# A four-layer vision kernel: the stage between two selective scans, with its turned images in a pool of their own

## Chip, cores and metric

The kernel runs on 1 core of one Trainium2 chip. The metric is the device time of one execution in microseconds (us), the median of several runs; lower is better.

## What is computed

The input is `x`, 4 images of 64 x 64 pixels with 192 channels, in float32. Four layers are applied in turn, each as `x = x + layer(group_norm(x))`. Layers 0 and 3 are two-dimensional selective scans ("ss2d"); layer 1 is a Mamba block over rows and columns, layer 2 a Toeplitz mixer. The change lies in layers 0 and 3. Cut to what matters, layer 0 is (layer 3 is the same with 192 instead of 384 inner channels):

```python
xz = x @ in_proj_w.T
xp, z = xz[..., :DI], silu(xz[..., DI:])
xc = silu(depthwise_conv3x3(xp) + conv_b)         # the "u" of the scans
xs = [rows(xc), columns(xc), reversed rows, reversed columns]
delta = softplus(...);  Bs, Cs = ...               # small projections of xs
h = exp(delta * A) * h + (delta * u) * B           # along 4096 positions, 16 states
y = sum over states of h * C, + D * u
y = y of the four ways, each turned back, summed
y = layer_norm(y) * gamma + beta
out = (y * z) @ out_proj_w.T
```

## The kernel before

**Layout.** An image lies as 96 partitions x 2 x 4096 pixels (`x`), the inner channels as `P` partitions x `NT` tiles: 128 x 3 in layer 0, 96 x 2 in layer 3. A chunk is `T` = 512 pixels, 8 rows; an image has `NCH` = 8 chunks.

**Order of the work.** `build` computes `both_weights` (weights of layer 1 multiplied out: 24 products on TensorE, stored to DRAM), then layer 0, layer 1, layer 2, layer 3. In each of layers 0 and 3, `ss2d` runs five "between" stages and four scans in turn: `ss2d_between(b)` makes the input of image b beside the output of image b-1, then `ss2d_scan` scans image b. The first between stage has no output, the last no input.

**Who orders instructions.** The kernel is written with a tile framework: the program says which tile each instruction reads and writes, pools give tiles their places in on-chip memory, and a planner orders each engine's instructions beforehand and puts in the waits. Each engine then runs its list strictly in order; SyncE (SP) and ScalarE and GpSimd hold DMA queues that are lists of the same kind. Pools are stacked from the left end of memory, or from the right one with `side="right"`; a pool that is closed leaves its place to later ones, which have to wait until its tiles are done with.

**Input** (`ss2d_input`, L550-645). Pool "a" on the left holds `pad`, the image with a border. Pool "a_u" (on the left behind it) holds `by_col`, the turned image of one tile (one buffer, 16 KB per partition), `one` (4 buffers of 2 KB) and `o` (2 of 16 KB). Pool "a_x" on the right holds `x`. `x` is loaded (L570), normalised (L103) and projected on TensorE (`in_ps`, L593) into `pad` (L597). Then the convolution: the last tile by nine products per chunk on TensorE (`conv_ps`, L612), Silu (`one`, L614), turned on GpSimd (L615); the other tiles by nine passes on VectorE (`o`, L622 and L624), Silu (L627), turned as a whole on GpSimd (L632). Rows go to DRAM as `u_d[0]` (L616, L628), the turned image as `u_d[1]` from SP's queue (L635). The turned image of tile NT-2, the last one made, is stored by a function `late` that `ss2d_input` returns.

**Output** (`ss2d_output`, L736-820), eight chunks from the last to the first. Pool "o_in" on the right (2 buffers) holds `acc` (the row result of the scans), `u` and `xr`, the image; `cols` on the left holds all column results. Its own tiles lie in pools "o", "o_stats" and "o_turn" on the left, where "a" and "a_u" were. Per chunk:

- `xn` is `xr` normalised (L103), `z` its projection (`zp`, L760) through Silu (L764)
- `acc` gets D times `u` (L766) and the columns (L771)
- the mean over channels is a product (`mean`, L774); it is subtracted from `acc` in place (L775); Square into `sq` (L777, 2 buffers), `var` (L780), then Ln and Exp (L782, L783)
- `acc` is scaled, shifted and gated in place (L784, L786, L789)
- the output product (`op`, L794) reads `acc`, and `xo` (L797) adds `xr`
- `xo` is stored (L798); in layer 0 it is also turned on GpSimd (`turned`, L802) for layer 1
- the loads of the chunk two further on are issued (`fetch`, L61)

In layer 0, for images 0 and 1, the statistics of image b+2 are counted here too, in four loads of 1024 pixels (`peek`, L812, 2 buffers; `count`, L77).

**Scan** (`ss2d_scan`). For each of four ways and each chunk it loads `u` from `u_d[col]`, projects it (`xd_ps`, L226) and scans (VectorE, L428/L435; products with C on GpSimd, L439). The ways come in the order columns, rows, columns reversed, rows reversed; the reversed ways add what the forward ones stored (`earlier`).

Of the kernel before, what the change touches and what calls it, by code (L numbers as in the profile page):

```python
# [7 lines left out]
F32 = mybir.dt.float32  # L8
AF = mybir.ActivationFunctionType
# [5 lines left out]
C = 192  # L15
# [21 lines left out]
class Kernel:  # L37
# [436 lines left out]
    def ss2d(self, pre, x_in, x_out, P, NT, ways, bias_twice, counted, turn):  # L474
# [4 lines left out]
        with tc.tile_pool(name=f"{pre}lay", bufs=1) as lay:  # L479
            w = {"counted": counted, "turn": turn}  # L480
            for name in ("in_w", "conv_w", "conv_b"):
                w[name] = self.load(lay, name, ins[pre + name])
            taps = w["taps"] = lay.tile([P, 9, P], F32, name="taps")
            w["nm"] = lay.tile([PC, B, KC, 2], F32, name="nm")
            A = self.load(lay, "A", ins[f"{pre}A"])
            D = self.load(lay, "D", ins[f"{pre}D"])
            dtb = self.load(lay, "dtb", ins[f"{pre}dt_b"])
            for name in ("gamma", "beta", "out_w"):
                w[name] = self.load(lay, name, ins[pre + name])
            avg = w["avg"] = lay.tile([P, P], F32, name="avg")  # L490
# [12 lines left out]

            for b in range(B + 1):
                self.ss2d_between(b, x_in, x_out, u_d, y_d, P, NT, w, begin if b == 0 else None)
                if b < B:
                    self.ss2d_scan(pre, u_d[b], y_d[b], P, NT, ways, A, dtb)

    def ss2d_between(self, b, x_in, x_out, u_d, y_d, P, NT, w, begin):
# [3 lines left out]
        with ExitStack() as ctx:  # L513
# [25 lines left out]
            if b < B:  # L539
                late = self.ss2d_input(b, x_in, u_d[b], P, NT, w, begin, ahead)  # L540
            else:
                ahead()
                late = None
            if last is not None:
                self.ss2d_output(last, x_in, x_out[last], P, NT, w, cols, loads, late)
            elif late is not None:
                late()
            aside.close()

    def ss2d_input(self, b, x_in, u_d, P, NT, w, begin, ahead):  # L550
# [5 lines left out]
        with (  # L556
            tc.tile_pool(name="a", bufs=1) as pa,
            tc.tile_pool(name="a_u", bufs=2) as pu,
            tc.tile_pool(name="a_ps", bufs=4, space=PSUM) as psum,
# [6 lines left out]
            with tc.tile_pool(name="a_x", bufs=1, side="right") as px:  # L566
# [22 lines left out]
                for t in range(NT):  # L589
                    for c in range(NCH):  # L590
# [9 lines left out]
                        )  # L600
            ahead()
            for t in [NT - 1, *range(NT - 1)]:
                by_col = pu.tile([P, HW, HW], F32, name="by_col", bufs=1)
                turned = by_col.rearrange("p b a -> p a b")
                bias = cb[:, t : t + 1]
                if t == NT - 1:
                    for c in range(NCH):
                        rows = slice(c * ROWS, (c + 1) * ROWS)
                        ps = psum.tile([P, ROWS, HW], F32, name="conv_ps", tag="mm")
                        for j in range(9):  # L610
                            win = pad[:, t, c * ROWS + j // 3 : (c + 1) * ROWS + j // 3, j % 3 : j % 3 + HW]
                            nc.tensor.matmul(ps, taps[:, j, :], win, start=j == 0, stop=j == 8)  # L612
                        one = pu.tile([P, ROWS, HW], F32, name="one", bufs=4)
                        nc.scalar.activation(one, ps, AF.Silu, bias=bias)  # L614
                        nc.gpsimd.tensor_copy(turned[:, rows, :], one)  # L615
                        nc.sync.dma_start(u_d[0][:, t, c * T : (c + 1) * T], one.rearrange("p a b -> p (a b)"))  # L616
                else:
# [14 lines left out]
                    nc.gpsimd.tensor_copy(turned, o)  # L632

                def late(t=t, by_col=by_col):
                    nc.sync.dma_start(u_d[1][:, t, :], by_col.rearrange("p a b -> p (a b)"))  # L635

                if t != NT - 2:
                    late()
            if fresh:
# [4 lines left out]
                self.moments(nm[:, 1], self.mv[:, 1], pa, psum)  # L644
        return late

    def ss2d_scan(self, pre, u_d, y_d, P, NT, ways, A, dtb):
# [3 lines left out]
        with (  # L651
# [26 lines left out]

            for k, (col, rev) in sorted(enumerate(ways), key=lambda one: (one[1][1], not one[1][0])):
                w = {"dtb": dtb[:, k, :], "A": A[:, k]}  # L680
# [54 lines left out]

    def ss2d_output(self, b, x_in, x_out, P, NT, w, cols, loads, late):  # L736

# [4 lines left out]
        with (  # L742
# [8 lines left out]
            for at, c in enumerate(range(NCH - 1, -1, -1)):  # L751
# [21 lines left out]
                for t in range(NT):  # L773
                    nc.tensor.matmul(mean, avg, acc[:, t, :], start=t == 0, stop=t == NT - 1)  # L774
                nc.vector.tensor_sub(acc, acc, mean.unsqueeze(1).broadcast_to([P, NT, T]))  # L775
                sq = po.tile([P, NT, T], F32, name="sq")
                nc.scalar.activation(sq, acc, AF.Square)  # L777
                var = psum.tile([P, T], F32, name="var")
# [4 lines left out]
                nc.scalar.activation(rstd, rstd, AF.Exp, scale=-0.5)  # L783
                nc.vector.tensor_mul(acc, acc, rstd.unsqueeze(1).broadcast_to([P, NT, T]))  # L784
                for t in range(NT):
                    nc.scalar.activation(  # L786
                        acc[:, t, :], acc[:, t, :], AF.Identity, bias=be[:, t : t + 1], scale=g[:, t : t + 1]
                    )
                nc.vector.tensor_mul(acc, acc, z)  # L789
                xo = po.tile([PC, KC, T], F32, name="xo")  # L790
                for m in range(KC):
                    op = psum.tile([PC, T], F32, name="op", tag="op")
                    for t in range(NT):
                        nc.tensor.matmul(  # L794
                            op, ow[:, t, m * PC : (m + 1) * PC], acc[:, t, :], start=t == 0, stop=t == NT - 1
                        )
# [9 lines left out]
                if at + 2 < NCH:  # L806
                    loads["fetch"](c - 2)
                if at == 0 and late is not None:
                    late()
# [12 lines left out]
    def both_weights(self):  # L822

        nc, ins = self.nc, self.i
        P, NT = 128, 3
        both_w = [self.dram.tile([P, NT, C], F32, name=f"m_both_w{i}") for i in range(4)]
        with (
            self.tc.tile_pool(name="n", bufs=2) as pn,
            self.tc.tile_pool(name="n_ps", bufs=2, space=PSUM) as psum,
        ):  # L830
            fw = self.load(pn, "fw", ins["L1_fc_w"], bufs=1)
            for i, part in enumerate((4, 6, 0, 2)):
# [9 lines left out]
                nc.sync.dma_start(both_w[i], both)  # L842
        return both_w

# [368 lines left out]
def build(tc, ins, out):  # L1213
    with ExitStack() as ctx:
        k = Kernel(ctx, tc, ins, out)
        x0 = [ins["x"][b] for b in range(B)]
        x1, x3 = (k.image_tiles(n) for n in ("x1_", "x3_"))
        both_w = k.both_weights()
        turned = k.image_tiles("turned")
        k.ss2d("L0_", x0, x1, 128, 3, ROW_COL, False, False, turned)  # L1220
        k.toeplitz(x1, k.mamba(x1, turned, both_w), x3)
        k.ss2d("L3_", x3, [out[b] for b in range(B)], 96, 2, ROW_ROW, True, True, None)
# [122 lines left out]
```

## Time and profile before

| | |
|---|---|
| median of 3 runs | 30774.61 us (30773.04 to 30777.48) |
| the profiled execution | 30801.53 us, its span 30799.7 us |
| granted TensorE clock in it | 0.963 of full speed |
| scans of layer 0 (first to last scan on VectorE) | 214-2496, 2882-5165, 5548-7828, 8186-10469 us |
| scans of layer 3 | 24844-26077, 26359-27592, 27875-29108, 29390-30624 us |
| convolution on TensorE (L612), each | 62 us |
| first to last `xo` of an output stage | 164 to 180 us in layer 0, 116 to 118 us in layer 3 |

A row of a list of groups or a timeline reads: engine, line, operation, output<-inputs, shapes; times are in us, a mean in ns. A row of waits reads: who waited at which line, "<-" for what, then the total, the times and the longest. In rows of stretches, each engine has its busy time and number of instructions; PEclk is the granted TensorE clock. PE is TensorE, DVE VectorE, ACT ScalarE, POOL GpSimd, SP SyncE; a "q" behind a name is its queue, PEld the weight loads.

### The profile page before, as it was taken

Reading aid. Unit: us, or ns where it says so; the run is one execution under the profiler, and the core shown is the slowest. Engines: PE = TensorE matmul, PEld = TensorE weight load, DVE = VectorE, ACT = ScalarE, POOL = GpSimd, SP = SyncE. Lnnn points to the kernel's source line nnn. Section 1 sums busy time; section 2 is a strip of 40 time slices with the busy share of each in tenths; the row PEclk is TensorE's granted clock in tenths of the full one; section 3 lists DMA queues with packets and bytes.
Section 4 is the critical chain, followed back from the end, with each engine's and each line's share of the span. In section 5 each row is a group of like instructions: output and inputs, shape, how many; then the busy total and the mean of one; then the engine's idle time right before and its main releaser. Section 6 shows DMA issues by size and latency. Waiting matters only on the chain. (4 is left out here: it accounts for less than half of the span.)

```text
span 30799.7 us, 503679 instructions
## 1 busy us (share of the span) xinstructions
PE 26995.3 (88%) x189440; PEld 15772.5 (51%) x189440; DVE 22446.6 (73%) x16865; ACT 23230.3 (75%) x50324; POOL 22912.2 (74%) x9903
## 2 busy tenths in 40 slices
PE   8998998899899888888888888888588988888888
PEld 5664665566466444444444444444355445444444
DVE  7886888788788677777777777777433367676777
ACT  6885886788688688888888888888222278888888
POOL 6885886788588599989998999999100068787877
PEclk9999999999999999999999999999788999999999
DMA  3333333333333333333333333333533445454444
GB/s 108 97 105 112 96 103 112 101 98 104 112 96 102 106 97 97 98 99 101 101 103 98 97 97 98 101 101 101 132 83 72 110 116 135 123 135 124 131 126 126
DMA packets 1644091, 3276.35 MB, mean 106 GB/s; under 512 B 395797, under 2 KB 452566, under 8 KB 1627574
## 3 DMA queue, kind: packets, MB, share of 16 engines
q1 hardware_dynamic: 1533110, 3076.28, 36.7%
q10 hardware_dynamic: 108544, 167.85, 1.6%
q8 instruction: 1497, 24.53, 0.3%
q14 instruction: 940, 7.70, 0.1%
HBM read 2121.50 MB, written 618.33 MB: 89 GB/s over the span
## 5 line engine op out<-in xcount | busy, mean ns | idle before, releaser
L395 PE MATMUL b<-diag,dtuT 128*64 128x256 f32 x98304 | 12600.0, 386 | 1753.8 <-DVE h L428 928.1
L439 POOL TENSOR_TENSOR hc<-h,c 128x1024 f32<-128x1024 f32 x4608 | 10947.5, 2395 | 2001.2 <-DVE h L435 1401.3
L395 PEld LDWEIGHTS b<-diag,dtuT 128*64 128x64 f32 x98304 | 8177.8, 138 | 6281.2 <-DVE h L428 1920.3
L418 ACT ACTIVATE dA<-both,A 128x512 f32<-128x512 f32 (+1 forms) x12288 | 8304.6, 716 | 2111.5 <-DVE h L428 1462.7
L435 DVE TENSOR_TENSOR_SCAN h<-dA,carry,b 128x512 f32<-128x512 f32 x6720 | 8170.0, 1264 | 1355.5 <-PE b L395 827.8
L439 POOL TENSOR_TENSOR h<-h,c 128x1024 f32<-128x1024 f32 x3072 | 7221.2, 2373 | 1058.6 <-DVE h L428 884.4
L349 ACT ACTIVATE diag<-ident,bt 128x128 f32<-128x128 f32 x20480 | 6617.8, 396 | 91.9 <-issue 91.3
L464 PE MATMUL y<-hc,fold 128*64 128x512 f32 x18432 | 5771.0, 599 | 383.9 <-POOL hc L439 382.2
L428 DVE TENSOR_TENSOR_SCAN h<-dA,b 128x1024 f32<-128x1024 f32 x2304 | 5204.5, 2275 | 1147.2 <-ACT dA L418 801.2
L368 POOL TENSOR_TENSOR bs<-dtu,bc 128x1024 f32<-128x1024 f32 x1536 | 3640.1, 2370 | 46.2 <-DMA c<-bc_dram 33.2
L464 PE MATMUL y<-h,fold 128*64 128x512 f32 x12288 | 3256.3, 593 | 8.9 <-POOL h L439 8.9
L464 PEld LDWEIGHTS y<-hc,fold 128*64 128x64 f32 x18432 | 1897.3, 138 | 1576.9 <-POOL hc L439 812.2
L428 DVE TENSOR_TENSOR_SCAN h<-b,bs 128x1024 f32<-128x1024 f32 x768 | 1759.1, 2290 | 1028.2 <-ACT b L418 728.9
L418 ACT ACTIVATE b<-both,A 128x504 f32<-128x504 f32 (+1 forms) x3072 | 2087.6, 680 | 360.0 <-DVE h L435 322.1
L563 POOL MEMSET pad<- 128x396 f32 (+1 forms) x8 | 7.7, 967 | 3093.3 <-DMA in_w<-in_L_in_w 2997.8
L435 DVE TENSOR_TENSOR_SCAN h<-b,carry,bs 128x512 f32<-128x512 f32 x1344 | 1639.9, 1261 | 234.4 <-issue 131.0
L254 PEld LDWEIGHTS dtu_ps<-ident,dtu 128*64 128x64 f32 (+1 forms) x16384 | 1173.6, 141 | 491.4 <-issue 365.3
L464 PEld LDWEIGHTS y<-h,fold 128*64 128x64 f32 x12288 | 1007.2, 137 | 787.2 <-issue 444.6
L435 DVE TENSOR_TENSOR_SCAN h<-dA,b 128x512 f32<-128x512 f32 x960 | 1112.1, 1206 | 374.2 <-PE b L395 196.2
L418 ACT ACT_TABLE_LOAD x1019 | 1307.4, 1283 | 13.3 <-DMA c<-bc_dram 1.6
L254 PE MATMUL dtu_ps<-ident,dtu 128*64 128x128 f32 (+1 forms) x16384 | 1263.0, 272 | 45.5 <-DVE dtu L295 41.2
L937 DVE SCALAR_TENSOR_TENSOR u<-in_ps,conv_w,u 128x504 f32<-128x504 f32 (+2 forms) x1152 | 832.5, 723 | 405.9 <-ACT u L932 396.8
(165 smaller groups left out, 25106.1 us busy)
## 6 DMA issues: line engine op xcount, KB each, us to landing
c<-bc_dram SPq DMA_DIRECT2D x3072, 256.0 KB, 4.1
both<-delta SPq DMA_DIRECT2D x2048, 128.0 KB, 2.8
bc<-bc_dram SPq DMA_DIRECT2D x768, 256.0 KB, 4.1
both<-delta_dram SPq DMA_DIRECT2D x1536, 128.0 KB, 3.5
dtu<-dtu_dram SPq DMA_DIRECT2D x1536, 128.0 KB, 2.6
dtu<-dtu SPq DMA_DIRECT2D x1280, 128.0 KB, 2.5
L_y<-out ACTq DMA_DIRECT2D x512, 256.0 KB, 3.1
u<-L_u SPq DMA_DIRECT2D x160, 768.0 KB, 5.5
```

Source lines behind the costliest of these rows:

```text
L254: nc.tensor.matmul(to[half * 64 : (half + 1) * 64], of[:, half * 64 : (half + 1) * 64], self.ident[:p, :p], start=True, stop=True,)
L349: nc.scalar.activation(to, self.ident, AF.Copy, scale=of)
L368: self.nc.gpsimd.tensor_mul(by(b), dtu, by(job["bbc"][p]))
L395: nc.tensor.matmul(to, dtu, job["diag"][p][:, k, 2 * q : 2 * q + 2, :], start=True, stop=True,)
L418: nc.scalar.activation(to[n], of, AF.Exp, scale=w["A"][:, g, 2 * p + n : 2 * p + n + 1])
L428: nc.vector.tensor_tensor_scan(h[:, way], dA[:, way], b[:, way], 0.0, ALU.mult, ALU.add)
L435: nc.vector.tensor_tensor_scan(hn[:, n, way], dA[:, n, way], by_n[:, n, way], start, ALU.mult, ALU.add)
L439: nc.gpsimd.tensor_mul(hc, h, job["cbc"][p])
L464: nc.tensor.matmul(y[c * 64 : (c + 1) * 64, :], self.fold, of, start=first == 0 and n == 0, stop=last == LAST and n == 1)
L563: nc.gpsimd.memset(pad[:, :, 0 : S : S - 1, :], 0.0)
L937: nc.vector.scalar_tensor_tensor(u[:, :, to], ps[:, :, of], tap(3 - j), u[:, :, to], ALU.mult, ALU.add)
```

## The change

- `a_u` is opened on the right side, after `ahead()` has opened "o_in" there; `one` has 3 buffers instead of 4.
- The turned images are stored from GpSimd's queue, each as soon as it is made; `late` is gone.
- The centred sum is a tile `yc` of its own (2 buffers); `acc` is no more written after the mean. `sq` has one buffer.
- `peek` is one buffer of 512 pixels, loaded eight times, one or two chunks per output chunk.
- The ways are ordered rows, columns, columns reversed, rows reversed.
- `both_weights` runs after the first between stage of layer 0 instead of ahead of it, in a pool on the right.

```diff
             for b in range(B + 1):
                 self.ss2d_between(b, x_in, x_out, u_d, y_d, P, NT, w, begin if b == 0 else None)
+                if b == 0 and turn is not None:
+                    self.both_weights()
...
-            tc.tile_pool(name="a_u", bufs=2) as pu,
...
             ahead()
+            pu = right.enter_context(tc.tile_pool(name="a_u", bufs=2, side="right"))
...
-                        one = pu.tile([P, ROWS, HW], F32, name="one", bufs=4)
+                        one = pu.tile([P, ROWS, HW], F32, name="one", bufs=3)
...
-                def late(t=t, by_col=by_col):
-                    nc.sync.dma_start(u_d[1][:, t, :], by_col.rearrange("p a b -> p (a b)"))
-
-                if t != NT - 2:
-                    late()
+                nc.gpsimd.dma_start(u_d[1][:, t, :], by_col.rearrange("p a b -> p (a b)"))
...
-            for k, (col, rev) in sorted(enumerate(ways), key=lambda one: (one[1][1], not one[1][0])):
+            for k, (col, rev) in sorted(enumerate(ways), key=lambda one: (one[1][1], one[1][0] != one[1][1])):
...
-                nc.vector.tensor_sub(acc, acc, mean.unsqueeze(1).broadcast_to([P, NT, T]))
-                sq = po.tile([P, NT, T], F32, name="sq")
-                nc.scalar.activation(sq, acc, AF.Square)
+                yc = po.tile([P, NT, T], F32, name="yc")
+                nc.vector.tensor_sub(yc, acc, mean.unsqueeze(1).broadcast_to([P, NT, T]))
+                sq = po.tile([P, NT, T], F32, name="sq", bufs=1)
+                nc.scalar.activation(sq, yc, AF.Square)
...
-                nc.vector.tensor_mul(acc, acc, rstd.unsqueeze(1).broadcast_to([P, NT, T]))
+                nc.vector.tensor_mul(yc, yc, rstd.unsqueeze(1).broadcast_to([P, NT, T]))
...
-                nc.vector.tensor_mul(acc, acc, z)
+                nc.vector.tensor_mul(yc, yc, z)
...
-                if at == 0 and late is not None:
-                    late()
-                if peek is not None and at < NCH // 2:
-                    one = po.tile([PC, KC, 2 * T], F32, name="peek")
-                    nc.sync.dma_start(one, x_in[peek][:, :, 2 * at * T : 2 * (at + 1) * T])
-                    for i in range(2):
-                        self.count(ahead, one[:, :, i * T : (i + 1) * T], 2 * at + i)
-                elif peek is not None and at == NCH // 2 + 1:
+                for i in () if peek is None else (0, 1) if at == 0 else (at + 1,) if at < NCH - 1 else ():
+                    one = po.tile([PC, KC, T], F32, name="peek", bufs=1)
+                    nc.sync.dma_start(one, x_in[peek][:, :, i * T : (i + 1) * T])
+                    self.count(ahead, one, i)
+                if peek is not None and at == NCH - 2:
                     self.sum_up(self.mv[:, peek], ahead)
...
-            self.tc.tile_pool(name="n", bufs=2) as pn,
+            self.tc.tile_pool(name="n", bufs=2, side="right") as pn,
...
-        both_w = k.both_weights()
```

More of the change, by code (lines that the diff above doesn't have):

```diff
@@ L539, in ss2d_between @@
             if b < B:
-                late = self.ss2d_input(b, x_in, u_d[b], P, NT, w, begin, ahead)
+                self.ss2d_input(b, x_in, u_d[b], P, NT, w, begin, ahead)
             else:
                 ahead()
-                late = None
             if last is not None:
-                self.ss2d_output(last, x_in, x_out[last], P, NT, w, cols, loads, late)
-            elif late is not None:
-                late()
+                self.ss2d_output(last, x_in, x_out[last], P, NT, w, cols, loads)
             aside.close()
@@ L644, in ss2d_input @@
                 self.moments(nm[:, 1], self.mv[:, 1], pa, psum)
-        return late
     def ss2d_scan(self, pre, u_d, y_d, P, NT, ways, A, dtb):
@@ L734, in ss2d_scan, with ss2d_output @@
             self.run_jobs(jobs, pools)
-    def ss2d_output(self, b, x_in, x_out, P, NT, w, cols, loads, late):
+    def ss2d_output(self, b, x_in, x_out, P, NT, w, cols, loads):
         tc, nc = self.tc, self.nc
@@ L783, in ss2d_output @@
                 nc.scalar.activation(rstd, rstd, AF.Exp, scale=-0.5)
-                nc.vector.tensor_mul(acc, acc, rstd.unsqueeze(1).broadcast_to([P, NT, T]))
+                nc.vector.tensor_mul(yc, yc, rstd.unsqueeze(1).broadcast_to([P, NT, T]))
                 for t in range(NT):
                     nc.scalar.activation(
-                        acc[:, t, :], acc[:, t, :], AF.Identity, bias=be[:, t : t + 1], scale=g[:, t : t + 1]
+                        yc[:, t, :], yc[:, t, :], AF.Identity, bias=be[:, t : t + 1], scale=g[:, t : t + 1]
                     )
-                nc.vector.tensor_mul(acc, acc, z)
+                nc.vector.tensor_mul(yc, yc, z)
                 xo = po.tile([PC, KC, T], F32, name="xo")
@@ L794, in ss2d_output @@
                         nc.tensor.matmul(
-                            op, ow[:, t, m * PC : (m + 1) * PC], acc[:, t, :], start=t == 0, stop=t == NT - 1
+                            op, ow[:, t, m * PC : (m + 1) * PC], yc[:, t, :], start=t == 0, stop=t == NT - 1
                         )
@@ L807, in ss2d_output @@
                     loads["fetch"](c - 2)
-                if at == 0 and late is not None:
-                    late()
-                if peek is not None and at < NCH // 2:
-                    one = po.tile([PC, KC, 2 * T], F32, name="peek")
-                    nc.sync.dma_start(one, x_in[peek][:, :, 2 * at * T : 2 * (at + 1) * T])
-                    for i in range(2):
-                        self.count(ahead, one[:, :, i * T : (i + 1) * T], 2 * at + i)
-                elif peek is not None and at == NCH // 2 + 1:
+                for i in () if peek is None else (0, 1) if at == 0 else (at + 1,) if at < NCH - 1 else ():
[3 more added lines that the diff above has]
+                if peek is not None and at == NCH - 2:
                     self.sum_up(self.mv[:, peek], ahead)
@@ L825, in both_weights @@
         P, NT = 128, 3
-        both_w = [self.dram.tile([P, NT, C], F32, name=f"m_both_w{i}") for i in range(4)]
+        both_w = self.both_w = [self.dram.tile([P, NT, C], F32, name=f"m_both_w{i}") for i in range(4)]
         with (
-            self.tc.tile_pool(name="n", bufs=2) as pn,
+            self.tc.tile_pool(name="n", bufs=2, side="right") as pn,
             self.tc.tile_pool(name="n_ps", bufs=2, space=PSUM) as psum,
@@ L842, in both_weights @@
                 nc.sync.dma_start(both_w[i], both)
-        return both_w
     def mamba(self, x_in, by_col, both_w):
@@ L1217, in build @@
         x1, x3 = (k.image_tiles(n) for n in ("x1_", "x3_"))
-        both_w = k.both_weights()
         turned = k.image_tiles("turned")
         k.ss2d("L0_", x0, x1, 128, 3, ROW_COL, False, False, turned)
-        k.toeplitz(x1, k.mamba(x1, turned, both_w), x3)
+        k.toeplitz(x1, k.mamba(x1, turned, k.both_w), x3)
         k.ss2d("L3_", x3, [out[b] for b in range(B)], 96, 2, ROW_ROW, True, True, None)
```

## The prediction

> **What bounds the kernel now.** I read the page first, for where time is lost at all.
>
> ```profile
> PE 26995.3 (88%) x189440; PEld 15772.5 (51%) x189440; DVE 22446.6 (73%) x16865; ACT 23230.3 (75%) x50324; POOL 22912.2 (74%) x9903
> ```
>
> Every engine is busy most of the time because the scans fill 27 of 30.8 ms. The change leaves the scans' instructions alone; it touches the stages between them. So I split the span by the first and last scan of each image in the timeline: in layer 0 DVE scans nothing in 0-214, 2496-2882, 5165-5548, 7828-8186 and 10469-10775 us; in layer 3 in 26077-26359, 27592-27875, 29108-29390 and from 30624 to the end, 30800. These holes (and the start of layer 3, 24697-24844) are what the change can win or lose: some 2500 us.
>
> Next, one hole in stretches: layer 0, input of image 1 beside output of image 0.
>
> ```profile
> core 0: us, PE busy (x) PEld busy (x) DVE busy (x) ACT busy (x) POOL busy (x), PEclk, DMA share, GB/s
> 2546.00:2608.00 62.00, 62.00 (x145) 27.01 (x143) 61.97 (x20) 14.26 (x13) 19.05 (x7) 1.00 0.43 142
> 2608.00:2649.00 41.00, 5.48 (x13) 2.20 (x12) 4.38 (x3) 0.69 (x1) 15.24 (x3) 0.60 0.56 227
> 2693.00:2739.00 46.00, 37.92 (x74) 14.63 (x73) 26.64 (x25) 21.13 (x24) 3.66 (x4) 0.87 0.27 84
> 2739.00:2800.00 61.00, 43.65 (x78) 16.54 (x77) 29.84 (x28) 23.05 (x26) 7.77 (x4) 0.78 0.24 75
> ```
>
> The convolution (row 1) fills PE. Then 41 us in which PE works 5.5. Then the output's eight chunks, in pairs of 46 to 61 us, where no engine is full and PE is nearest. The waits of 2608-2650 name the owner of the dead stretch:
>
> ```profile
> ACT sq L777 <- DMA L_u<-by_col: 40.5, 1, 40.5
> DVE xn L103 <- DMA L_u<-by_col: 33.4, 1, 33.4
> POOL by_col L632 <- DMA L_u<-by_col: 18.7, 2, 12.3
> ```
>
> xn and sq do not read by_col; they wait because their pool "o" lies on the place of the closed pool "a_u". by_col has one buffer, so the end is a serial chain on POOL: store, copy 7.08 us, store, copy, store. Tiles at the bottom of "o" wait too, although only its top reaches a_u, so the wait is by pool. The check: in layer 0's third hole (no peek tile, "o" 16 KB smaller, ending inside the old pad) the first zp starts at 7943.7, right after the convolution's 7942.3. There is no stall there.
>
> The two starts, from the waits of 150-214 and 0-45 us:
>
> ```profile
> PE xd_ps L226 <- DMA u<-L_u: 40.4, 1, 40.4
> DVE stats L77 <- DMA m_both_w<-both_w: 27.5, 1, 27.5
> ```
>
> The first scan reads turned columns, stored last (u loaded at 186.65); and the first statistics wait until both_weights' pool is free. Last, a pair of layer 3's output, from the timeline:
>
> ```profile
> 27776.49 0.31 SPq L61 DMA_DIRECT2D acc<-L_y  x1
> 27780.05 0.75 DVE L766 SCALAR_TENSOR_TENSOR acc<-u,Dsum,acc 96x512 f32<-96x512 f32 x1 [0.29 <-DMA acc<-L_y]
> 27784.16 1.99 PE L774 MATMUL mean<-acc,avg 96*96 96x512 f32 x2 [3.40 <-issue]
> 27792.28 1.22 DVE L775 TENSOR_TENSOR acc<-acc,mean 96x1024 f32<-96x1024 f32 x1 [1.22 <-PE mean L774]
> 27807.10 6.85 PE L794 MATMUL op<-acc,out_w 96*96 96x512 f32 x8 [5.92 <-DVE acc L789]
> ```
>
> acc's slot is free only when op has read it, so the load of the chunk two on is issued at op's end, and load, sum, mean (15.8 us to the subtraction at 27792.28) stand in series with the rest of every pair.
>
> **The change, part by part.**
>
> *By_col on the right (own pool, GpSimd stores).* From the tile sizes in KB per partition, layer 0: base 16, cols 48, pad 52 end at 116. The new "o" (xn 8, z 12, yc 12, sq 6, rstd 4, xo 8, peek 4) runs from 64 to 118. From the top: o_in 32, a_u 54 (by_col 16, one 6, o 32). With about 208 KB usable (the Trainium skill, "SBUF — State Buffer", section "SBUF size: 192, 224, or 256?"; no row shows it) a_u is 122 to 176: clear of "o". Layer 3: "o" ends near 82, a_u starts near 130. So the wait goes; next late is the convolution itself. What it is worth: from the convolution's end to the first op, holes 1 and 2 of layer 0 take 67.0 us (2608.1 to 2675.1), hole 3 takes 28.6 (7942.3 to 7970.9): 38.4 each, 77. In layer 3 it is 42.0, 42.0 and 40.9; without the wait, the 18.6 from xn to op (26198.7 to 26217.3) plus 4.5 of mean and subtraction that now sit inside the stall, about 23.5: 18 each, 55.
> Turned (32 KB on top of "o") still meets a_u, so GpSimd's first L802 waits for the last store, about 2650; xo is first due near 2642 and its buffer again a pair (42 us) later, so nothing waits. Bounds for this part: 132 gained, or 100 if the first output pair is slowed by DVE's tail.
>
> *Stores on GpSimd's queue.* SP's issue of one costs 0.32 us and it lands 6.3 us later (2 MB); three stores (layer 3: two) leave SP in each hole, worth about 1 us. Behind GpSimd's store stand only the next by_col copy, which needs that store anyway, and turned. No row shows a GpSimd store. A rule speaks against it: the Trainium skill, "SBUF — State Buffer", section "SBUF: two separate sides", says that such a store's descriptors are written by GpSimd, which is locked out while DVE runs a two-port operation. The nearest row: GpSimd's by_col copy takes 1.04 us alone and up to 5.27 beside DVE's taps (one tap pass 4.47). In the holes the first such store comes after DVE's taps (2600.7 against 2610.0), so row and rule both give 0; only at layer 0's start could it wait, some 4.5 us a store, and there rows go first. I take 0; bounds -2 and +5 a hole.
>
> *Right-hand a_u over x.* At layer 0's start peek holds the top 32 KB, so a_u lies on x, and in layer 3 o_in is only 24 KB. By the pool-wide wait above, DVE's taps now start when in_ps ends: +26.7 us at layer 0's start (61.8 to 88.5), +13 in layer 3. In layer 3 the convolution covers it (taps would end at 26157, PE at 26175). At layer 0's start it is not covered.
>
> *both_weights moved, rows first.* Start of layer 0: without the 27.5 us wait, the statistics follow x (its last part took 17 us from issue in hole 1, behind some 4 us of weight loads), ending near 27 instead of 38.65: 12 earlier. in_ps ends 76.5, taps (78.7 us, 61.8 to 140.5) end 155, Silu of the first rows and their store make u loadable at about 160.5 instead of 186.65: 26 gained. The moved 24 products (6.3+5.9 us of PE), 12 copies and 9 DMAs fit in PE's idle stretch from 138 to 165; with that cover gone they cost 12. Bounds 12 and 43 (if o's tiles miss x). Start of layer 3: u loadable when pad is free, about 24796 instead of 24819.3: 23. In the later holes the first u load (2812.23) waits for cols, not for by_col: order changes nothing there.
>
> *yc.* acc is free after the subtraction, so the next load, sum and mean lie beside Ln, Exp and op. Taking those 15.8 us out of layer 3's 37.4 us pair gives 21.6, but PE is busy 26 to 28 us in such a pair, so I take 29. Four outputs of three pair steps: 111.7, 111.8, 113.7 and 112.7 now, 87 then: 102. Layer 0: fetch to subtraction is 29.8 us (2777.05 to 2806.83), steps sum to 151, 147, 162 and 162; PE is busy 38 to 44 in a pair, so 42: 126 each, 118 in all. One sq buffer holds the second Square until var of the first, some 3 us, beside PE's work. xr is not freed earlier; z is needed last, so I cost it at 0 (5 a pair if not). Bounds: nothing, or 170 + 140 if PE at its full clock sets the pace (it is granted only 0.78 to 0.87 now).
>
> *Peek in eighths, one buffer.* Each of eight SP loads waits for DVE's count of the one before; DVE's count work (5.4 us) is the same. 0; up to 10 a hole, in two holes.
>
> **Sum.** 26 + 77 + 118 + 23 + 55 + 102 = 401. The profiled execution took 30801.5 us (span 30799.7 and 1.8 around it), 27 above the median 30774.6; 30400 by its own time, 30374 against the median.
>
> **Rivals.**
> - *Only the stalls go.* The instruction order is planned beforehand; if SP still has the next acc load behind the previous x store, or z's late xr holds the pair, the loop keeps its length: 26+77+23+55 = 181, so 30594. For it: xr and SP's one queue. Against: SP now issues acc first, 0.7 us ahead of the store.
> - *The overlap stays* (my addresses are off): 401 - 132 = 269, 30506. For it: I infer the layout. Against: hole 3.
> - *Slower: the freed front part runs too early.* If sum and mean of the next pair are queued on DVE and PE ahead of the current pair's var and op, in-order engines wait there for a load (5.1 us to land), sum and mean: up to 14 us a pair, over 24 steps 336, minus 181: +155, 30930. It decides from 7.5 us a pair on. The 13.8 us that a mean waits behind the other chunk's op (2789.4 to 2803.2) show that such order costs; that PE has gaps of 8 to 17 us a pair speaks against.
>
> **Chances.** My forecast 0.57 (30240 to 30480, the better bound included), only stalls 0.26, overlap stays 0.06, near no change 0.05, slower 0.06. The range 30240 to 30610 takes the first three. About 0.2% is what a measurement of this kernel can tell from no change: faster 0.90, same 0.04, slower 0.06.
>
> **What would show it.** No wait of xn or sq on by_col; first op 24 to 29 us after the convolution in every hole; pair steps of 42 and 29; acc issued before op; first u load near 160 and 24796; taps of layer 0's start beginning only at in_ps's end. I am wrong if pair steps stay at 50 and 37, or if by_col's stores on GpSimd take much longer than 7 us.

## The result, and the profile after

The changed kernel takes 30427.3 us (median of 4 runs, 30423.1 to 30431.7) against 30776.0 us for the kernel before (median of 4 runs, 30773.0 to 30782.8): a ratio of 0.9886, 95% interval 0.9869 to 0.9904. It is faster by 349 us, where 401 were forecast, and its time lies in the predicted range, 53 us above the predicted time. The profiled execution has a span of 30421.3 us against 30799.7, so the two traces lie 378 us apart.

Cut into the same pieces as in the prediction, the two traces give this ledger (us; "first op" is counted from the convolution's end, "loop" runs from the first xo of an output to the seventh chunk's, "tail" from there to the last xo, each summed over the outputs):

| piece | before | after | gained | forecast |
|---|---|---|---|---|
| layer 0, begin to first scan | 214.0 | 211.1 | 2.9 | 26 |
| layer 0, first op in holes 1, 2, 3 | 67.1, 67.0, 28.6 | 54.2, 53.4, 39.2 | 15.9 | 77 |
| layer 0, four loops | 621.9 | 441.1 | 180.8 | 118 |
| layer 3, convolution to first scan | 49.3 | 37.5 | 11.8 | 23 |
| layer 3, first op in three holes | 42.1, 42.1, 40.8 | 31.3, 31.4, 31.3 | 31.0 | 55 |
| layer 3, four loops | 449.8 | 295.9 | 153.9 | 102 |
| tails, both layers | 85.0 | 107.1 | -22.1 | 0 |
| the rest, scans included | | | 4.2 | 0 |

So the sum is nearly right and its terms are not: the loops gave half as much again as forecast, the stalls and the starts about a third of what was forecast for them.

The waits of layer 0's first hole after (2600 to 2665 us; total, times, longest) answer to those shown of before:

```profile
ACT sq L771 <- DVE yc L769: 21.1, 2, 10.8
POOL by_col L631 <- DMA L_u<-by_col: 19.7, 2, 11.2
DVE stats L77 <- DMA peek<-in_x: 17.8, 3, 11.3
DVE acc L759 <- DMA acc<-L_y: 10.8, 2, 6.0
```

No wait of xn or sq on by_col is left; only the next copy waits for by_col's store, as it must. But VectorE now waits for the peek and for an acc load, and Square waits for VectorE. A pair of layer 3 after, from the timeline:

```profile
26025.20 1.22 DVE L769 TENSOR_TENSOR yc<-acc,mean 96x1024 f32<-96x1024 f32 x1 [0.76 <-PE mean L767]
26026.44 0.31 SPq L61 DMA_DIRECT2D acc<-L_y  x1
26028.49 3.60 PE L788 MATMUL op<-yc,out_w 96*96 96x512 f32 x8
```

acc's load is issued as the subtraction ends, ahead of op, where before it followed op. The pair steps of this loop are 20.3, 31.3 and 21.4 us, for 36.4, 37.7 and 37.6. Its stretches in one table, after first, then two pairs of before:

```profile
core 0: us, PE busy (x) PEld busy (x) DVE busy (x) ACT busy (x) POOL busy (x), PEclk, DMA share, GB/s
26003.00:26023.00 20.00, 18.56 (x43) 6.50 (x42) 16.55 (x20) 15.53 (x18) 0.00 (x0) 1.00 0.55 158
26023.00:26054.00 31.00, 26.62 (x58) 9.28 (x56) 18.99 (x22) 19.11 (x23) 0.00 (x0) 0.94 0.44 120
26054.00:26076.00 22.00, 19.65 (x40) 6.68 (x40) 11.10 (x14) 15.66 (x18) 0.00 (x0) 0.92 0.24 72
```

```profile
26225.00:26261.00 36.00, 26.40 (x48) 8.50 (x46) 17.76 (x21) 19.04 (x21) 0.00 (x0) 0.81 0.31 87
26261.00:26299.00 38.00, 27.70 (x49) 9.38 (x50) 18.41 (x22) 19.04 (x21) 0.00 (x0) 0.78 0.30 83
```

PE's busy time in a pair was 26 to 28 us at a granted clock of about 0.8; after it is 19 to 27 at 0.92 to 1.00, 21.6 in the mean of the three. Times clock, that is 21 to 22 us for a pair of before and 20.6 after, for about as many instructions (48 and 47 a pair), so the floor that the prediction took (PE's busy time of before) was for the most part a product of the lower clock. PE now fills 86 to 93% of each stretch, more than any other engine, so most likely it sets the pace of the loop; no run tested that.

### The profile page after: what moved, and what is told of

Same layout as the page of the kernel before. It is cut to its first block, busy times and chain, and to the rows that moved or that the text cites. A ratio compares the mean times of both kernels' runs of the same rounds, so it can differ in the third digit from the quotient of the medians.

```text
span 30421.3 us, 503594 instructions
## 1 busy us (share of the span) xinstructions
PE 26912.4 (88%) x189440; PEld 15805.4 (52%) x189440; DVE 22493.1 (74%) x16865; ACT 23137.3 (76%) x50306; POOL 22960.8 (75%) x9923
```

## Experiments

All twelve runs, in us. "First op" is the median hole of its kind (holes 1 and 2; hole 3; layer 3), "loops" the sums of four. Each ratio is to the kernel before as timed in the same series. That kernel had medians of 30768 to 30779 in the three series, so a difference of 10 us between medians of two kernels says little, and the pieces of the traces decide. Every run of e7, e9, e10, e11 and e12 was faster than every run of the changed kernel, and every run of e1, e2 and e13 slower; the runs of e3, e4, e5 and e6 overlap with it, so that these four are read from their traces alone.

| run | time | ratio to before, 95% interval | first op | loops |
|---|---|---|---|---|
| before | 30776.0 | 1 | 67, 28.6, 42.1 | 622, 450 |
| after | 30427.3 | 0.9886 (0.9869 to 0.9904) | 54, 39.2, 31.3 | 441, 296 |
| e1_yc_alone | 30551.4 | 0.9929 (0.9914 to 0.9944) | 68, 38.9, 42.7 | 465, 311 |
| e2_without_yc | 30660.7 | 0.9965 (0.9952 to 0.9978) | 43, 28.6, 20.9 | 634, 443 |
| e3_turn_on_act | 30414.7 | 0.9887 (0.9870 to 0.9903) | 50, 43.9, 27.5 | |
| e4_weights_at_start | 30441.1 | 0.9893 (0.9878 to 0.9908) | | |
| e5_peek_later | 30416.7 | 0.9886 (0.9871 to 0.9900) | 55, 38.6, 31.4 | 441, 297 |
| e6_columns_first | 30435.4 | 0.9890 (0.9874 to 0.9907) | | |
| e7_stores_by_sp | 30388.8 | 0.9874 (0.9860 to 0.9889) | 41, 39.2, 25.5 | 430, 302 |
| e9_copies_in_eighths | 30391.7 | 0.9876 (0.9861 to 0.9891) | 55, 34.3, 23.1 | 449, 295 |
| e10_left_at_starts | 30396.7 | 0.9878 (0.9863 to 0.9893) | 54, 39.5, 31.3 | 444, 297 |
| e11_together | 30379.5 | 0.9871 (0.9857 to 0.9886) | 55, 33.8, 23.5 | 443, 298 |
| e12_no_peek | 30402.6 | 0.9879 (0.9862 to 0.9895) | 39, 38.6, 31.4 | 451, 293 |
| e13_three_sums | 30506.8 | 0.9912 (0.9897 to 0.9927) | 69, 41.7, 31.2 | 462, 334 |

**The two halves.** The first run is the kernel before with yc and one sq buffer, the second the changed kernel with acc centred in place.

```diff
 e1, on before                            e2, on after: the same lines back
-nc.vector.tensor_sub(acc, acc, mean...)
+yc = po.tile([P, NT, T], F32, name="yc")
+nc.vector.tensor_sub(yc, acc, mean...)
...
-op, ow[:, t, m * PC : (m + 1) * PC], acc[:, t, :]
+op, ow[:, t, m * PC : (m + 1) * PC], yc[:, t, :]
```

> The kernel before with one part of the change: the centred sum in a tile yc of its own, one sq buffer. Theory (the shorter output loop carries nearly all of the gain): four output loops of each of layers 0 and 3 shrink as in the changed kernel, first to last pair from some 155 to some 110 us in layer 0 and from 112 to 74 in layer 3, so 300 to 340 us less than before, about 30450, with the waits on by_col's store unchanged. Rival (the stalls carry it, and the loop shortens only when its start is free of them): under 150 us less, over 30620.

> The changed kernel with the centred sum back in place in acc and two sq buffers. Theory (the pool on the right, rows first and the moved weights together bring little, since the turned copies now run beside the output): 30 to 70 us less than before, about 30725; the first op 40 to 55 us after the convolution in layer 0. Rival (as predicted, the stall's removal and the starts are worth 181 us): about 30595.

yc alone gained 217 us, everything else alone 108; together they make 325 of the 349, so in the total they nearly add up. Neither expectation was met: each run lies between its theory and its rival. The traces say why. With yc alone the loops shrink by 157 and 139, nearly as in the change, but hole 3's first op comes 10 us later (28.6 to 38.9) and layer 3's tails grow from 3.9 to 19 in each of three holes. Without yc the stall is fully gone in layer 3 (first op at 20.9, even before the 23.5 of the forecast) and more than half gone in holes 1 and 2. Beside e2 the changed kernel has its first op some 10.5 us later in every one of the six holes. So yc shortens the loop and delays its beginning.

**The whole-image copy.** In hole 3 after, the order of VectorE, and beside it GpSimd (start, us, engine, line, operation, operands, idle time before it):

```profile
7840.11 1.75 DVE L769 TENSOR_TENSOR yc<-acc,mean 128x1536 f32<-128x1536 f32 x1 [6.39 <-PE mean L767]
7847.95 5.89 DVE L759 SCALAR_TENSOR_TENSOR acc<-u,Dsum,acc 128x512 f32<-128x512 f32 x3 [6.09 <-DMA acc<-L_y]
...
7858.20 1.76 DVE L778 TENSOR_TENSOR yc<-yc,rstd 128x1536 f32<-128x1536 f32 x1
7864.18 3.63 DVE L759 SCALAR_TENSOR_TENSOR acc<-u,Dsum,acc 128x512 f32<-128x512 f32 x1 [4.22 <-issue]
7867.73 1.74 DVE L783 TENSOR_TENSOR yc<-yc,z 128x1536 f32<-128x1536 f32 x1
```

```profile
7844.88 7.24 POOL L631 COPY by_col<-o 128x4096 f32<-128x4096 f32 x1 [11.46 <-DMA L_u<-by_col]
...
7860.20 7.20 POOL L631 COPY by_col<-o 128x4096 f32<-128x4096 f32 x1 [7.26 <-DMA L_u<-by_col]
```

A sum (L759) takes 0.74 us alone. The three that begin inside the first copy take 5.89 together and end after it (copy until 7852.12); the one inside the second takes 3.63 and ends at 7867.81, where the copy ends at 7867.40. VectorE's operation with two inputs sits out the rest of GpSimd's copy. The Trainium skill states this as a rule (page "SBUF — State Buffer", section "Who interferes with whom"): a VectorE instruction with two inputs in on-chip memory and a GpSimd one that reads on-chip memory exclude each other, and the later one is blocked until the earlier is done. The trace agrees. In holes 1 and 2 and in layer 3 this copy ran before while the output was stalled; the change put it beside the output. In hole 3, which had no stall, it ran beside the output before too, and the trace of before shows the same hold on a product with rstd that took 1.78 us for the chunk before:

```profile
7970.73 7.22 POOL L632 COPY by_col<-o 128x4096 f32<-128x4096 f32 x1 [6.40 <-DMA L_u<-by_col]
7973.85 5.56 DVE L784 TENSOR_TENSOR acc<-acc,rstd 128x1536 f32<-128x1536 f32 x1 [4.00 <-ACT rstd L783]
```

Two runs move the copy:

```diff
 e3
-nc.gpsimd.tensor_copy(turned, o)
+nc.scalar.copy(turned, o)
 e9
-nc.gpsimd.tensor_copy(turned, o)
+for c in range(NCH):
+    rows = slice(c * ROWS, (c + 1) * ROWS)
+    nc.gpsimd.tensor_copy(turned[:, rows, :], o[:, rows, :])
```

> The changed kernel with the whole-image turned copies on ScalarE instead of GpSimd. Theory (GpSimd's 7.2 us copy holds up VectorE's sums of two inputs from on-chip memory while it runs): no sum at L759 over 1.5 us after the convolution, and the first op comes some 29 us after the convolution in layer 0's third hole (39 in the changed kernel) and 24 in layer 3's (31), so 40 to 70 us less than the changed kernel, about 30370. Rival (the sums are slow because their inputs still land, or the copy only moves its cost to another engine that the output needs): 30427 within 15 us, or more.

> The changed kernel with GpSimd's whole-image copy cut into eight copies of 8 rows each. Theory (VectorE's two-input sums are held until a copy that runs on GpSimd ends; an eighth holds them 0.9 us and not 7.2): no sum at L759 over 3 us after the convolution, first op some 33 us after the convolution in layer 0's third hole (39 in the changed kernel) and 26 in layer 3's (31), together 30 to 45 us less than the changed kernel, about 30390. Rival (the first pair is late because VectorE's list puts the next pair's sums, and so their loads, ahead of it): within 10 us of 30427.

The sums (min, median and max in ns) over all of after, then in hole 3 with the copy on ScalarE (7835 to 7890 us) and in eighths (the same window; L761 is their line there):

```profile
L759 DVE SCALAR_TENSOR_TENSOR acc<-u,Dsum,acc x160: 724/742/6220, 2580.0 to 30371.2; 128x512 f32<-128x512 f32 x96, 96x512 f32<-96x512 f32 x64
```

```profile
L759 DVE SCALAR_TENSOR_TENSOR acc<-u,Dsum,acc x11: 747/752/1384, 7838.3 to 7883.3; 128x512 f32<-128x512 f32 x11
```

```profile
L761 DVE SCALAR_TENSOR_TENSOR acc<-u,Dsum,acc x6: 752/1390/1401, 7853.3 to 7874.0; 128x512 f32<-128x512 f32 x6
```

Off GpSimd, no sum is held after the convolution (the 1.38 us fall inside it), so the copy was the cause of the hold. In eighths the copy costs the sums little, at most 1.42 us in any hole after the convolution. The first op of layer 3 comes at 23.1, near the 23.5 that the prediction forecast, and 36 us are won. (In all three kernels one sum of 3.9 us is left, at the start of layer 3's last output, where no copy of by_col runs but GpSimd's last products of the last scan.) On ScalarE the copy takes as long as on GpSimd, and there Square and z of the output stand behind it:

```profile
L631 ACT COPY by_col<-o x12: 7092/7216/7300, 157.6 to 28911.2; 128x4096 f32<-128x4096 f32 x8, 96x4096 f32<-96x4096 f32 x4
```

So the cost moved from one engine to the other: the first op of hole 3 comes later (43.9), and the medians differ by 13 us, within what the runs leave open.

**The peek.** In holes 1 and 2 the counts of the peek stand on VectorE ahead of the first subtraction. One run issues the peek a chunk later in the code, the other leaves out the statistics of images 2 and 3 (their loads and counts; image 1's moments stand in).

```diff
 e5
-for i in () if peek is None else (0, 1) if at == 0 else (at + 1,) if at < NCH - 1 else ():
+for i in () if peek is None or at == 0 else (0, 1) if at == 1 else (at,):
...
 e12
-    self.count(ahead, one, i)
...
-    self.moments(nm[:, peek], self.mv[:, peek], ps1, psum, tag="op")
+    nc.vector.tensor_copy(nm[:, peek], nm[:, 1])
```

> The changed kernel with the eight peek loads and counts one output chunk later (two at the second chunk, then one each). Theory (in layer 0's holes 1 and 2 the counts of peek stand on VectorE's list ahead of the first subtraction and wait there for their load): the first op comes some 39 us after the convolution in holes 1 and 2, as in hole 3, instead of 54, so about 28 us less than the changed kernel, near 30400. Rival (the counts only move, or the first pair is held by the sums of the next one anyway): 54 within 4 us, 30427 within 8.

> The changed kernel without the statistics of images 2 and 3 in layer 0: their loads and counts are left out and image 1's moments stand in. Theory: in holes 1 and 2 three counts stand on VectorE ahead of the first subtraction and wait for their loads (the wait's row: 17.8 us in three waits); without them the first op comes about as in hole 3, 39 us after the convolution instead of 54 and 53, and the loops of these holes (109) keep their length: 30 us less, 30397. Rival: the later arrival in holes 1 and 2 has another cause (the turned copy and the order of the pairs' work, which holes 1 and 2 share with hole 3 only in part): under 10 us less, first op still after 48.

Without the statistics the first op comes at 39.0 and 38.9, as in hole 3: the 15 us of difference are theirs, and 25 us are won in the median (9 to 12 in a hole by the trace, since the loops get a few us longer). Moving them in the code did nothing (55): VectorE's waits for the peek are those of after (17.9 us in three waits, the longest 11.3). The order of the instructions is planned beforehand; the planner placed the counts ahead of the subtraction again.

**The order on VectorE.** In the hole-3 lines above, the sums of the third chunk stand ahead of the first chunk's product with rstd (L778), and the first sum of the fourth ahead of its product with z (L783), and they wait for loads; this is the mechanism of the prediction's rival "Slower". A third buffer for acc, loaded one chunk further ahead, asks whether the wait or the order is the price (where its expectation says "pair", it is the third chunk that is meant):

```diff
+early = {}
+def ys(c):
+    src = y_d[last][0][:, c * T : (c + 1) * T].rearrange("(t p) l -> p t l", p=P)
+    return self.load(po, "acc", src, bufs=3)
...
-self.load(po, "acc", y_d[last][0][:, s].rearrange("(t p) l -> p t l", p=P)),
+early.pop(c) if c in early else ys(c),
...
```

> The changed kernel with a third buffer for acc, loaded one pair further ahead. Theory (the wait is the price): VectorE stood 7.8 and 4.2 us at the start of hole 3's loop on the third pair's load with the first pair's product and scale behind it; with the load three pairs ahead this wait is gone: first op 5 to 10 us earlier in each of seven holes, 30370 to 30395. Rival (the order is the price): VectorE has the later pair's sums ahead of the first pair's work whether they wait or not, so each still costs its 5 to 10 us of VectorE's time and the first op comes as late as now: 30427 within 10 us.

It lost 79 us. The third chunk's sums now ran during the convolution, and the fourth chunk's took their place: in layer 3 the first op stayed at 31.2, in holes 1 and 2 it came at 69. Later in the same loop (layer 3, VectorE):

```profile
26043.20 6.56 DVE L767 SCALAR_TENSOR_TENSOR acc<-u,Dsum,acc 96x512 f32<-96x512 f32 x2 [4.00 <-DMA acc<-L_y]
...
26060.34 1.41 DVE L767 SCALAR_TENSOR_TENSOR acc<-u,Dsum,acc 96x512 f32<-96x512 f32 x2 [6.40 <-DMA acc<-L_y]
26061.67 1.22 DVE L791 TENSOR_TENSOR yc<-yc,z 96x1024 f32<-96x1024 f32 x1
...
26111.74 1.00 DVE L103 TENSOR_SCALAR xn<-xr,nm 96x512 f32<-96x512 f32 x2 [5.93 <-DMA xr<-x]
26112.65 1.21 DVE L786 TENSOR_TENSOR yc<-yc,rstd 96x1024 f32<-96x1024 f32 x1
```

Sums and normalisations of chunks to come stand waiting for their loads, with products of the current chunk behind them. With one buffer more, the planner put that work further ahead. The theory (the wait) fell; the rival had the mechanism but not the size, since it expected no loss.

**The queue of the stores.** by_col's stores on SyncE's queue again:

```diff
-nc.gpsimd.dma_start(u_d[1][:, t, :], by_col.rearrange("p a b -> p (a b)"))
+nc.sync.dma_start(u_d[1][:, t, :], by_col.rearrange("p a b -> p (a b)"))
```

> The changed kernel (30427.3) with one edit: the three stores of a turned image are issued by SyncE's queue again. Theory: that GpSimd issues them is worth nothing by itself, since the image's copy is what the next one waits for: 30427 within 10 us, and first op 54, 53, 39 and 31 us after the convolution as before. Rival 1: SP's stores landed sooner (6.3 us in the trace of before, 8.3 us by GpSimd's queue after), and three of them stand one behind another in a stage: 2 us each where the chain binds, about 20 us less at the two starts (the diagonal matrices wait for the last store there). Rival 2: SP stands waiting for a copy with the loads of the next pair behind it: 20 to 60 us more, first op later than 39 in hole 3.

It gained 38 us between the medians (24 between the spans). The theory and the second rival missed; the first rival named about 20, but for the starts and for stores that land sooner, and neither is so (issue to landing of SyncE's stores in this run):

```profile
DMA to landing us min/median/max: 6.3/8.4/13.3
```

By GpSimd's queue it was 6.6, 8.3 and 11.9. Two other things differ. In layer 3 it is the planned order, here in the first hole, after first, then this run:

```profile
25992.85 1.41 DVE L759 SCALAR_TENSOR_TENSOR acc<-u,Dsum,acc 96x512 f32<-96x512 f32 x2 [6.45 <-DMA acc<-L_y]
25994.18 1.22 DVE L783 TENSOR_TENSOR yc<-yc,z 96x1024 f32<-96x1024 f32 x1
```

```profile
25965.68 1.22 DVE L783 TENSOR_TENSOR yc<-yc,z 96x1024 f32<-96x1024 f32 x1 [1.59 <-ACT yc L780]
25971.55 1.22 DVE L778 TENSOR_TENSOR yc<-yc,rstd 96x1024 f32<-96x1024 f32 x1 [4.65 <-ACT rstd L777]
```

After, the first chunk's product with z stands behind a later chunk's sums and their load; here it does not, and the first op comes 5 to 6 us sooner. In holes 1 and 2 it comes 12 to 14 us sooner, and 9 to 10 of these are won before the order of the products matters: the first subtraction comes 11.1 and 11.7 us after the convolution instead of 21.1 and 20.8. Only two counts of the peek stand ahead of it instead of four, and the peek's first load, issued at the convolution's end in both, is counted from 9.9 and 10.5 us after the convolution instead of 14.7 and 14.5. The first by_col store goes out some 2 us behind that load, here on the same queue, after on GpSimd's; that this is why the load lands sooner is what the times suggest, and no run separates it. In hole 3, with no peek, the order changed too, but the second copy held L783 for 6.24 us and the first op stayed at 39.2. Some of what holes 1 and 2 gain is given back in their tails (20 for 12). At layer 0's start the same edit costs 5 us (first scan at 216.0): the load of out_w stands on SyncE's queue behind a store that waits for its copy. Why the planner orders the two kernels differently was not taken apart.

**The starts.** At layer 0's start after, PE does this between the convolution and the first scan:

```profile
165.97 0.45 PE L95 MATMUL v<-dev,group 96*96 96x2 f32 x2 [25.65 <-DVE dev L93]
166.71 7.36 PE L829 MATMUL both_ps<-fw,ow 96*128 96x192 f32 x24 [0.30 <-DVE nm L97]
178.22 6.80 PE L829 MATMUL both_ps<-fw,ow 96*128 96x192 f32 x24 [4.15 <-DMA ow<-in_L_out_w]
185.43 1.52 PE L226 MATMUL xd_ps<-u,xw 128*64 128x256 f32 x12 [0.41 <-ACT both_w L832]
```

and SyncE's queue has (u is what the first scan reads):

```profile
155.09 7.89 SPq L627 DMA_DIRECT2D L_u<-o  x4
171.27 3.50 SPq L833 DMA_DIRECT2D m_both_w<-both_w  x2
174.86 0.87 SPq L61 DMA_DIRECT2D ow<-in_L_out_w  x2
175.90 0.59 SPq L61 DMA_DIRECT2D u<-L_u  x1
```

The first scan's xd_ps stands behind the moved weights' products on PE (24 products, 48 instructions), and its u behind their stores on SyncE's queue, which wait for ScalarE's copies of the products. The products in turn stand behind image 1's moments, one step of which (dev, 96 by 2) took 6.82 us at 158.81, inside a whole-image copy. Three runs change one thing each:

```diff
 e4
+            if turn is not None:
+                self.both_weights()
             for b in range(B + 1):
...
-                if b == 0 and turn is not None:
-                    self.both_weights()
 e6
-(one[1][1], one[1][0] != one[1][1])
+(one[1][1], not one[1][0])
 e10
-tc.tile_pool(name="a_u", bufs=2, side="right")
+tc.tile_pool(name="a_u", bufs=2, side="right" if begin is None else "left")
```

> The changed kernel with both_weights back ahead of layer 0's first stage, its pool still on the right. Theory (behind the convolution its 48 product instructions and 13 DMA and copy steps stand between the convolution and the first scan's projection): the first scan starts at about 195 us instead of 211, some 15 us less than the changed kernel. Rival (the first scan waits for DVE's taps and for the weights alike, or x comes later behind the weights' loads): 211 within 4 us.

> The changed kernel with the ways in the order of the kernel before (columns, rows, columns reversed, rows reversed). Theory (rows first lets the first scan begin before the turned images are stored): nothing in the holes between scans; layer 0's start some 14 us longer (u then waits for the last store, about 190 us), layer 3's some 20 us, so 30460. Rival A (the start waits for the scan's own pools, which lie on a_u and so wait for the last store anyway): both starts within 5 us. Rival B (the order changes the scans themselves): the scans of layer 0 change by over 5 us each.

> The changed kernel with a_u on the left side at the two starts alone (no output stands beside them). Theory (at the starts the right-hand a_u lies on x, so the taps wait for the projection, and the scan's diagonals lie on a_u, so they wait for the last turned store): the taps begin some 27 us earlier in layer 0, the first scan at about 178 us instead of 211, and layer 3's first scan some 25 us after its convolution instead of 37.5; 40 to 48 us less than the changed kernel, about 30383. Rival (both_weights and the statistics of image 1 hold the first scan): 211 within 8 us.

With the weights at the very start the convolution ends 8 us later (148.0 for 140.2), since x's loads queue behind theirs, and the first scan comes at 216.3: the move is worth about 5, by the trace. Columns first delays the first scan by 5 us and layer 3's by 12, and leaves the later holes as they are: that is what rows first is worth, 17 by the trace (its expectation said 34) and 8 between the medians, which the runs do not separate. Turned images on the left let the taps run from 51.1 to 129.8 instead of 78.6 to 158.7, and the first scan comes at 190.6, 20 us sooner; layer 3's start gains 6. Here the theory held in its mechanism; of the 33 us that it expected at layer 0's start 13 are missing: u was loaded at 141.1, ahead of the weights' stores this time, but xd_ps came at 160.4, right behind the products.

**Together.** The eighths, the left side at the starts, the weights issued right after image 1's loads, and the later peek:

> The changed kernel with what the single runs found, together: the whole-image copy in eighths (30392 alone, 36 less), turned images on the left at the two starts (30397 alone, 31 less), the weights' products issued as soon as image 1's loads are out (so that they don't stand ahead of layer 0's second convolution), and the peek a pair later (nothing by itself, 10 less by one reading). Theory: the parts act at different places, so they add: 67 less, and about 10 more from the weights' products; 30350, first scan at about 180, first op 23 after the convolution in layer 3. Rival: at the starts the eighths don't matter and the weights' loads delay x as they did in the run with them first (8 us): 30375.

It has the lowest median of all (its runs overlap with those of e7), 48 us below the change, but 29 above its theory and 4 above its rival (30375). At layer 0's start xd_ps began at 155.5 instead of 185.4, yet the first scan only at 195.2, for 190.6 with the left side alone. The convolution ended 7 us later (147.0), because the weights' instructions stand among the projections on PE (8.6 us, from 40 to 51), not because x came late as in e4; and on SyncE's queue the scan's loads of c wait 6.5 us for by_col's last store, until 193, when ScalarE also goes on to dA, for which the first scan waits. The holes of layer 3 got shorter as with the eighths alone (231.9 for 239.8); the peek stayed where it was (first op at 55). Stores on SyncE's queue were not tried with it.

## Why the prediction was right, and where its sum was off

The cause was right in both parts: yc takes load, sum and mean out of the pair's chain, and the pool's place was what made xn and sq wait. That the total came out within 52 us is luck: against the forecast the loops gave 115 more, the stalls 85 less, the starts 34 less and the tails 22 less. Two sums of the working are off and carry nothing: the stages that the change can touch add up to some 2800 us, not 2500, and the scans fill 25 of the 30.8 ms, not 27.

- **The loops (forecast 220, measured 335).** The step "PE is busy 26 to 28 us in such a pair, so I take 29" was mis-sized, and "42" in layer 0 with it. PE's busy time at a clock of 0.8 was taken as a floor; after it is 19 to 27 us in layer 3's pairs, at 0.92 to 1.00, and the step is 24.7 in the mean there (295.9 by twelve) and 36.8 in layer 0 (441.1 by twelve). The better bound (PE at its full clock, 170 + 140) was nearer than the forecast, and the loops passed even that by 25. What grants the higher clock was not tested.
- **What yc gives back (forecast 0).** "z is needed last, so I cost it at 0" looked for the cost in the wrong place. e2 against after, by traces: loops 340 gained, first ops 63 later in six holes, tails about 17 longer. That leaves 260; the spans differ by 238 and the medians by 233, near the forecast 220.
- **The stalls (forecast 132, measured 47 in the change, 110 in e2).** In layer 3 the miss of 8 us a hole is the copy beside the output (31.3 to 23.1 in e9), and it costs as much because it holds sums that stand ahead of the first chunk's products: with the order of e7 it is 25.5 under the same copy. In hole 3 it is 5 us of copy; the other 6 go with yc (28.6 in e2), most likely by the order. In holes 1 and 2 there are another 15 us from the peek, which "Peek in eighths: 0" put at nothing; the named bound of 10 a hole was about what e12 gave. That the copy could hold VectorE was weighed in the prediction only from the other side (VectorE's taps holding GpSimd), though hole 3 of before shows it (L784, 5.56 us).
- **The starts (forecast 49, measured 15).** Taps do begin only at in_ps's end (78.6 after 78.4) and the statistics end at 28.5, near the predicted 27. The step that failed is that the moved products "fit in PE's idle stretch from 138 to 165": they began at 166.7, behind the moments, and their stores put the load of u at 175.9 instead of 160.5; their second half held PE until 185.0, some 4 us after u had landed (a load of u takes 5.5 us). That is 19 of the 23 us missing here; the prediction counted PE's room for the step, not its place in SyncE's queue. At layer 3's start u was loaded at 24597.9, at the convolution's end, but the first diagonals came at 24627.3, when the last by_col store (issued at 24617.6) had landed. The profile names no releaser there. e10 shows the cause: with a_u on the left the store lands as late (29.2 us after the convolution, for 29.3), but the diagonals come 10.1 us after it instead of 29.5. So they waited for the place of a_u on the right. The first scan gains only 6 of these 19, since other work then holds it.
- **GpSimd's stores (forecast 0, bounds -2 and +5 a hole).** They land as SyncE's do in the median, and the wait that the prediction feared at layer 0's start did not come: the store issued at 146.1, beside VectorE's taps, took 0.74 us to issue and 6.7 to land. They cost 24 to 38 us all the same, in layer 3 by the planned order, in holes 1 and 2 for the most part at the peek (e7), and no view of the trace of before could show either.
- **The rivals.** "Only the stalls go" was the reverse of what happened. "The overlap stays" fell: no wait of xn or sq on by_col is left. "Slower" is real as a mechanism, about 10 us at the beginning of each output (and in e13 another 9 in each loop of layer 3), but not in each pair, where it needed 7.5 us: in the middle of the loop acc's loads arrive in time (from 26003 to 26076 VectorE waits for none of them, and 7.8 us for xr).

## What to carry to other kernels

Do not take an engine's busy time for a floor before looking at the clock that was granted while it was measured. When a stall goes, list what ran inside it at no cost: here a copy on GpSimd and a few counts on VectorE came to lie beside or ahead of the output's first work and took some 60 of 132 us back (8 in three holes and 5 in one, 15 in two). Where a planner orders the instructions, a spare buffer or another queue changes the order as well as the wait; run each such part alone before believing that it costs nothing.

## What the runs showed of the hardware

- Beside a whole-image copy on GpSimd (7.2 us) a 96 by 2 operation of VectorE took 6.82 us and a sum of 0.74 us up to 6.22; with the copy in eighths (1.07 us each in the median) no sum took over 1.42 us in the holes of e9 after the convolution, and with it on ScalarE none was held.
- ScalarE needed 7.2 us for the same copy with turned writing, no less than GpSimd.
- A store of a turned image (1.6 or 2.1 MB) landed in a median of 8.3 us from GpSimd's queue and of 8.4 from SyncE's, and in 6.3 us in the stalled first hole before; GpSimd's issue takes 0.53 us for SyncE's 0.32.
- A load of 0.4 MB (the first peek), issued by SyncE some 2 us ahead of such a store, was there for VectorE 14.4 to 15.1 us later in four kernels with the store on GpSimd's queue (after, e2, e5, e9; two holes each), and 9.8 to 10.4 us later in the one with the store on SyncE's (e7).
- The granted clock in a pair of the output was 0.78 to 0.81 when its steps took 37 us, and 0.92 to 1.00 when they took 20 to 31.
